# Moving 28 parts of a hand-written schedule: the scan layer's fronts, ends and early values, one at a time within or between its steps

## The chip, the cores and the metric

The kernel runs on one core of one Trainium2 chip. The metric is the device time of one execution in microseconds (us). The kernel before takes 5843.45 us, the median of three runs from 5842.38 to 5847.58. Engines are called as the profile calls them: PE (TensorE matmul; PEld is its weight load), DVE (VectorE), ACT (ScalarE), POOL (GpSimd) and SP, the queue that issues nearly all DMAs.

## The reference

Two layers in float32 on x, 4 images of 384 channels and 64x64 pixels. Each normalises its input in groups (32 groups) and adds its result to it: `x = x + layer(gn(x))`.

Layer 0 is a Mamba block on the 4096 tokens of an image. The change is in this layer:

```python
xn = (xs - mu) * rsqrt(var + 1e-05) * ln_w + ln_b
xb, z = split(xn @ in_proj_w.T)                 # 2 x 768 channels
xc = silu(causal_conv(xb, 4 taps) + conv_b)
dt, Bm, Cm = split(xc @ x_proj_w.T)             # 24, 16, 16
dt = softplus(dt @ dt_w.T + dt_b)
h_t = exp(dt_t * A) * h_(t-1) + (dt_t * x_t) * B_t   # 768 x 16 states, t = 0..4095
y_t = h_t . C_t
out = ((y + xc * D) * silu(z)) @ out_proj_w.T
```

Layer 1 is outlook attention with 3x3 windows at stride 2: attention weights from the pooled pixels, values from a 3x3 convolution, a weighted sum folded back, and a projection. A part of its values is computed early, between the steps of layer 0; that is all of it that the change touches.

## The kernel before

**Tiles and steps.** `mamba_layer` (line 111) cuts the 4 x 4096 tokens into 68 chunks of 241 tokens. One scan instruction covers 32 channels x 16 states (128 partitions, four stretches of 242 columns, 968 in all); a step of the main loop (line 956) has two of them, and 12 steps make a chunk's 768 channels. I number a chunk's steps 0 to 11. All chunks run as a pipeline: while a chunk's 12 steps scan, later chunks are prepared (fronts), an earlier one is finished (ends), and layer 1's early values are computed (behinds).

What a step does for the scan itself, in its order on each engine: SP fetches `dxr` and `dtr` for coming steps (even steps, `s_fetch` line 734 and `s_fetch_dt` line 743, four DMAs each); DVE writes half of the scan's input for the next step, `h<-dxr,bp` (`s_inputs2`, line 765), then runs two scans `h<-da,h` (`s_scan`, line 786); ACT copies the carried state (`s_carry`), makes the decays `da` of the next step in two groups of four exponentials (`s_decay`, line 774), each as soon as a scan has freed its buffer, and saves the state (`s_save`); POOL multiplies the scanned h of the step before by C, `h<-h,bc` (`s_outputs`, line 796), and writes the other half of the input two steps ahead, `h<-dxr,bc` (`s_inputs`, line 750); PE sums over states into y on odd steps (`s_sum`).

**What sets the order.** The order is written out by hand: each engine is wrapped in `InOrder` (line 38), which keeps its instructions in program order, so an instruction that waits holds everything behind it on its engine. Three tables say where other work goes. `plan` (line 608) holds the parts of a chunk's front, `ends` (line 642) its end, `behinds` (line 651) the early values. A key is a step, relative to the chunk, and one of six places in a step, EARLY, READY, SCAN, POOL, MID, LATE: before the next step's `h<-dxr,bp`; after it and before the scans; between the second scan and the second group of decays; after `h<-h,bc`; after `h<-dxr,bc` and PE's sum; last. Steps that differ by 12 fall on the same step of the loop for different chunks. `parts` (line 688) calls them, later chunks first. On an engine that a part doesn't use, its place means nothing; two places are the same for an engine that issues nothing between them.

**The parts** that matter below:

- the norm: `f_load`, `f_mean` (PE), `f_center` (DVE), `f_square` (ACT, line 312, 128x723), `f_var` (PE), `f_root` and `f_pow` (ACT: logarithm, then exponential, in place of a root), `f_scale` (DVE);
- projections and convolution: `f_x`, `f_z`, `f_conv` (PE, with ACT evictions), three of each; `f_gates` (ACT: two table loads and the Silu activations);
- `f_bc`, `f_xd` (line 447: ACT copies `xd`, SP stores it as `bcd`), `f_spread` (line 486: SP reads `bcd` back, eight DMAs), `f_dt`, `f_plog`, `f_log` (ACT), and `f_dtx` (line 512): DVE multiplies dt by xc for two of the six channel blocks, SP stores the product with four DMAs. Its tile has two buffers for three products of a chunk:

```python
def f_dtx(c, jj):
    if jj == 0:
        c.dxd = dram.tile([NJ, CG, 4, TM], F32, tag="dxd", name="dxd")
    dtx = front.tile([P, 2, TM], F32, tag="dtx", name="dtx", bufs=2)
    ve.tensor_mul(dtx, c.pl[jj], c.xc[jj][:, :, 1:])
    store(dtx, c.dxd[2 * jj : 2 * jj + 2])
```

- the ends: `e_load` (SP: `xr<-in_x`), `e_project` (PE and ACT: `ps_out`, `xr`), `e_mean`, `e_store` (SP: `x1<-xr`);
- the early values: `v_load` (line 534; SP loads the pixels of the next pair of tiles, `xo<-x1`, in three parts, in the chunk before the pair), `v_norm`, `v_begin`, `v_item` (PE `ps_v`, ACT `v<-ps_v`), `v_next` (line 596; SP stores `ve<-v` and fetches `wq`). Pairs of tiles start in chunks 20, 24, 28, 32, 37, 41, 45, 49, 54, 58 and 62 and last four chunks each.

Of the kernel before, what the change touches and what calls it, by code (L numbers as in the profile page):

```python
# [110 lines left out]
def mamba_layer(ctx, tc, x, w, x1, sc1, bi1, bi4, consts, early, behind):  # L111
# [410 lines left out]
    EARLY, READY, SCAN, POOL, MID, LATE = range(6)  # L522

    def at(f, *args):
        def part(c):
            f(c, *args)

        part.f = f
        return part
# [66 lines left out]
    def v_next(ch, n):  # L596
# [9 lines left out]
                    v_fetch(q + 1, cb)  # L606

    plan = {
        (-2, LATE): [f_load],
        (1, READY): [f_mean],  # L610
        (1, POOL): [f_center],
        (3, EARLY): [f_square],
        (3, POOL): [f_var],
        (3, LATE): [f_root],
        (4, READY): [f_pow],
        (4, POOL): [f_scale],
        (7, MID): [at(f_x, 0)],
        (8, EARLY): [at(f_x, 1)],
        (8, MID): [at(f_z, 0)],
        (9, MID): [at(f_conv, 0)],  # L620
        (10, SCAN): [at(f_z, 1)],
        (10, LATE): [at(f_z, 2)],
        (11, SCAN): [at(f_conv, 1)],
        (13, READY): [at(f_x, 2)],
        (13, MID): [at(f_conv, 2)],
        (13, LATE): [f_gates],
        (14, READY): [f_bc],
        (14, POOL): [f_xd],
        (15, SCAN): [at(f_dt, 0)],
        (15, POOL): [at(f_dt, 1)],  # L630
        (15, LATE): [f_column],
        (16, LATE): [at(f_dt, 2), at(f_plog, 0)],
        (17, EARLY): [f_spread],
        (17, LATE): [at(f_plog, 1)],
        (18, EARLY): [at(f_dtx, 0)],
        (18, READY): [at(f_plog, 2), at(f_dtx, 1), f_log],
        (19, READY): [at(f_dtx, 2)],
        (22, SCAN): [f_b],
        (25, LATE): [f_last],
    }  # L640

    ends = {
        (-4, SCAN): [lambda c: e_load(c)],
        (2, POOL): [lambda c: e_project(c, 0)],
        (5, MID): [lambda c: e_project(c, 1)],
        (6, SCAN): [lambda c: e_project(c, 2)],
        (7, READY): [lambda c: e_mean(c)],
        (7, MID): [lambda c: e_store(c)],
    }

    behinds = {
        (0, SCAN): [at(v_item, 0)],
        (1, READY): [at(v_next, 0)],
        (2, EARLY): [at(v_item, 1)],
        (3, POOL): [at(v_next, 1)],
        (4, SCAN): [at(v_item, 2)],
        (5, POOL): [at(v_next, 2)],
        (5, LATE): [at(v_item, 3)],
        (7, EARLY): [at(v_next, 3)],
        (8, SCAN): [at(v_load, 0)],  # L660
        (8, LATE): [at(v_item, 4)],
        (9, POOL): [at(v_load, 1)],
        (9, MID): [at(v_next, 4)],
        (10, READY): [at(v_load, 2)],
        (10, LATE): [at(v_norm, 0)],
        (11, EARLY): [v_begin],
        (11, MID): [at(v_norm, 1), at(v_norm, 2)],
    }

    def chunk(k):  # L670
# [160 lines left out]
    def e_tokens(c, v):  # L831

        return v[c.b, :, c.t0 - 1 + c.lo : c.t0 - 1 + TM].rearrange("(p cb) l -> p cb l", cb=NCB)

    def e_load(c):
        c.lo = 1 if c.ci == 0 else 0
        c.xr = io.tile([P, NCB, XT], F32, tag="xr", name="xr")
        sp.dma_start(c.xr[:, :, c.lo : TM], e_tokens(c, x))

    def e_project(c, cb):  # L840
        lo = c.lo
        po = pmm.tile([P, 2, TM], F32, tag="mm", name="ps_out")
        pe.matmul(po[:, 0, lo:], ident, c.xr[:, cb, lo:TM], start=True, stop=False)
        for j in range(NJ):
            pe.matmul(po[:, 0, lo:], wout[:, j, cb, :], c.zs[:, j, lo:TM], start=False, stop=(j == NJ - 1))
        if cb == 0:
            c.sums = small.tile([P, NCB], F32, tag="sums", name="sums")
        ae.activation(c.xr[:, cb, lo:TM], po[:, 0, lo:], AF.Identity, accum_out=c.sums[:, cb : cb + 1])

    def e_mean(c):  # L850


        n = TM - c.lo
        if c.ci == 0:
            st1[c.b] = small.tile([P, NC, 3], F32, tag="st1", name="st1")
            gp.memset(st1[c.b][:, 0:1, 0:1], float(NCB * n))
            gp.memset(st1[c.b][:, 1:, 0:1], float(NCB * TM))
        ae.activation(
            c.sums,
            c.sums,  # L860
            AF.Identity,
            scale=1.0 / (NCB * n),
            accum_out=st1[c.b][:, c.ci, 1:2],
        )

    def e_store(c):
        n = TM - c.lo
        ae.activation(
            c.zs[:, :NCB, :n],
            c.xr[:, :, c.lo : TM],  # L870
            AF.Square,
            scale=-1.0,
            bias=st1[c.b][:, c.ci, 1:2],
            accum_out=st1[c.b][:, c.ci, 2:3],
        )
        sp.dma_start(e_tokens(c, x1), c.xr[:, :, c.lo : TM])
        if c.ci == NC - 1:
            b = c.b
            made = group_norm_coeffs(
                pe, ve, ae, gp, small, pmm, blk4, mhalf, [st1[b].rearrange("p a s -> p (a s)")], sc1[:, b : b + 1], bi1[:, b : b + 1]  # L880
            )
            def parts():
                yield from made
                ae.mul(bi4[:, b : b + 1], bi1[:, b : b + 1], 4.0)

            norms.append([parts(), False])
# [655 lines left out]
def layers(ctx, tc, w, out):  # L1542
# [35 lines left out]

    started = []
    mamba_layer(tc, x.rearrange("b c h w -> b c (h w)"), w, x1, sc1, bi1, bi4, consts, early, behind)  # L1580
    outlook_layer(tc, x1, w, out, sc1, bi1, bi4, weights, ready, tiles)

# [67 lines left out]
```

## Time and profile before

| what | us |
|---|---|
| median of three runs | 5843.45 |
| the profiled execution, its own time | 5847.81 |
| its span | 5846.0 |
| first scan starts, last scan starts | 94.67, 4936.06 |
| one chunk, from first scan to first scan, chunks 1 to 19 (mean) | 70.6 |
| the same, the 40 chunks with early values under way (mean) | 71.3 |
| a scan on DVE, 128x968 | 2.15 |
| `h<-dxr,bp` on DVE, 128x964 | 1.13 |
| `dtx<-ps_lg,xc` on DVE, 128x482 | 0.65 |
| `h<-h,bc` on POOL, 128x1928 | 3.97 |
| `h<-dxr,bc` on POOL, 128x964 | 2.00 |
| four exponentials of `da` on ACT, 128x241 each | 1.62 |
| `sq<-u,bc` on ACT, 128x723 | 0.89 |

How to read it: the profile is one execution, taken by the hardware profiler. A row of a timeline says when an instruction started (us from the span's start), how long it took, its engine, and in square brackets how long the engine had been idle and what ended that. SPq rows are DMA issues, of which x4 means four in a row. A row of the waits view says who waited for whom: us in total, times, longest. All instructions that pass through `InOrder` carry its line, L53, so groups are told apart by their tiles.

### The profile page before, as it was taken

How to read it: one execution, taken by the hardware profiler on the slowest of the kernel's cores; microseconds unless marked ns; L12 is line 12 of the kernel's file. 1: busy time of each engine (PE TensorE's matmuls, PEld its weight loads, DVE VectorE, ACT ScalarE, POOL GpSimd, SP SyncE). 2: the span in 40 equal slices, each digit the busy share in tenths (PEclk: the TensorE clock that was granted, in tenths of full speed). 3: DMA queues.
4: the chain of work that ended last, by engine and by line, in shares of the span. 5: the costliest groups of instructions: out<-in, count | busy, mean ns of one | idle time of the engine just before them, and what ended most of it. 6: DMA issues, size and time to landing. Idle time of an engine off the chain costs nothing.

```text
span 5846.0 us, 126302 instructions
## 1 busy us (share of the span) xinstructions
PE 5294.4 (91%) x46156; PEld 3831.6 (66%) x46156; DVE 5248.9 (90%) x4267; ACT 4834.3 (83%) x13288; POOL 5404.3 (92%) x2051
## 2 busy tenths in 40 slices
PE   7888888888999999998999999999999996899999
PEld 6666666666666666666666666666666664567655
DVE  4999999999999999999999999999999998588644
ACT  4888888888888888888888888888889886577665
POOL 4999999999999999999999999999999998799733
PEclk9999999999999999999999999999999998999999
DMA  4555555555667666666666666656666656666554
GB/s 146 143 143 144 143 139 134 130 132 135 167 170 180 173 177 163 173 171 160 172 177 175 178 169 174 170 148 171 169 166 172 162 149 170 187 210 214 173 168 150
DMA packets 761512, 956.85 MB, mean 164 GB/s; under 512 B 211839, under 2 KB 663609, under 8 KB 760761
## 3 DMA queue, kind: packets, MB, share of 16 engines
q1 hardware_dynamic: 758296, 945.24, 59.6%
q8 instruction: 362, 5.93, 0.4%
q10 hardware_dynamic: 2592, 3.54, 0.2%
q14 instruction: 262, 2.14, 0.1%
HBM read 722.67 MB, written 225.70 MB: 162 GB/s over the span
## 4 chain that ended last, share of the span: by engine, by line
ACT 24%; PE 22%; DVE 8%; DMA 5%; POOL 4%; issue 4%; SPq 3%; ACTq 0%; DVEq 0%; POOLq 0%
ACT da L53 13%; DVE h L53 5%; PE ps_in L53 4%; PE ps_v L53 3%; SPq L53 3%; POOL h L53 3%; PE y L53 3%; PE psv L53 3%; PE ps L53 2%; PE pso L53 2%; PE psa L53 2%; PE ps_cv L53 2%; ACT L53 2%; DMA dtr<-dtd 1%; ACT xc L53 1%
## 5 line engine op out<-in xcount | busy, mean ns | idle before, releaser
L53 DVE TENSOR_TENSOR_SCAN h<-da,h 128x968 f32<-128x968 f32 x1632 | 3451.3, 2154 | 150.0 <-POOL h L53 73.5
L53 POOL TENSOR_TENSOR h<-h,bc 128x1928 f32<-128x1928 f32 x816 | 3240.9, 3972 | 41.5 <-DVE h L53 37.8
L53 ACT ACTIVATE da<-dtr,alog 128x241 f32<-128x241 f32 x6528 | 2644.7, 453 | 362.5 <-DVE h L53 290.1
L53 POOL TENSOR_TENSOR h<-dxr,bc 128x964 f32<-128x964 f32 x816 | 1633.2, 2001 | 57.3 <-issue 37.9
L53 PE MATMUL ps_in<-u,win 128*128 128x241 f32 x4824 | 1060.3, 371 | 44.7 <-ACT xb L53 28.9
L53 PEld LDWEIGHTS ps_in<-u,win 128*128 128x128 f32 x4824 | 907.0, 191 | 170.5 <-ACT xb L53 51.6
L53 DVE TENSOR_TENSOR h<-dxr,bp 128x964 f32<-128x964 f32 x816 | 925.2, 1134 | 4.9 <-DMA dxr<-dxd 3.6
L53 PE MATMUL y<-h,ssum 128*32 128x241 f32 x13056 | 777.8, 372 | 50.8 <-POOL h L53 50.7
L53 PE MATMUL ps_cv<-xb,cdiag 128*128 128x241 f32 x3264 | 718.7, 373 | 27.9 <-ACT zs L53 21.6
L53 PEld LDWEIGHTS ps_cv<-xb,cdiag 128*128 128x128 f32 x3264 | 606.5, 190 | 135.2 <-issue 34.8
L53 PEld LDWEIGHTS y<-h,ssum 128*32 128x32 f32 x13056 | 435.1, 111 | 317.9 <-POOL h L53 69.8
L53 POOL TENSOR_TENSOR bd<-ain,own 99x1188 f32<-99x1188 f32 x192 | 432.7, 2277 | 171.9 <-PE ps L53 156.9
L53 PE MATMUL ps_out<-zs,wout 128*128 128x241 f32 (+1 forms) x2448 | 564.4, 382 | 5.8 <-DVE zs L53 5.8
L53 ACT ACTIVATE bd<-ain,own 99x216 f32<-99x216 f32 (+1 forms) x1408 | 463.4, 417 | 92.1 <-PE ps L53 82.6
L53 PEld LDWEIGHTS ps_out<-zs,wout 128*128 128x128 f32 x2448 | 489.0, 200 | 49.1 <-DVE zs L53 6.2
L53 PE MATMUL ps_v<-wq,xo 128*32 128x384 f32 x4752 | 424.2, 489 | 31.9 <-ACT xr L53 30.1
L53 DVE TENSOR_TENSOR fold<-fold,ps 128x192 f32<-128x192 f32 (+1 forms) x768 | 210.1, 302 | 161.0 <-PE ps L53 136.5
L53 PE MATMUL ps_dt<-xd,wdt 128*128 128x241 f32 x816 | 227.6, 404 | 93.4 <-ACT xd L53 56.8
L53 PEld LDWEIGHTS ps_v<-wq,xo 128*32 128x32 f32 x4752 | 141.7, 110 | 238.2 <-issue 161.9
L53 PE MATMUL pso<-fold,wpr 128*128 128x256 f32 (+6 forms) x1026 | 279.4, 419 | 3.7 <-DVE fold L53 3.3
L53 PE MATMUL ps<-bd,vin 99*32 99x99 f32 (+1 forms) x9216 | 228.3, 250 | 43.6 <-DVE fold L53 20.4
L53 PEld LDWEIGHTS ps<-bd,vin 99*32 99x32 f32 (+1 forms) x9216 | 200.9, 110 | 98.2 <-issue 38.6
(132 smaller groups left out, 5554.6 us busy)
## 6 DMA issues: line engine op xcount, KB each, us to landing
dxr<-dxd SPq DMA_DIRECT2D x1632, 120.5 KB
dtr<-dtd SPq DMA_DIRECT2D x1632, 120.5 KB
wq<-in_wv SPq DMA_DIRECT2D x297, 192.0 KB
dxd<-dtx SPq DMA_DIRECT2D x816, 60.2 KB
dtd<-dt SPq DMA_DIRECT2D x272, 180.8 KB
ve<-v SPq DMA_DIRECT2D x198, 192.0 KB
bc<-bcd SPq DMA_DIRECT2D x272, 120.5 KB
vin<-ve SPq DMA_DIRECT2D x66, 445.5 KB
```

The lines of the kernel that those rows point to most:

```text
L53: made = self.tc.keep_in_program_order(issue(*args, **kwargs))
```

## The change

Only the three tables change: 28 entries stand at other places, and `f_root` shares one with `f_pow`. No instruction is added, removed or altered. The whole diff of the tables:

```diff
     plan = {
-        (-2, LATE): [f_load],
-        (1, READY): [f_mean],
+        (-1, EARLY): [f_load],
+        (0, LATE): [f_mean],
         (1, POOL): [f_center],
-        (3, EARLY): [f_square],
+        (2, POOL): [f_square],
         (3, POOL): [f_var],
-        (3, LATE): [f_root],
-        (4, READY): [f_pow],
-        (4, POOL): [f_scale],
+        (4, READY): [f_root, f_pow],
+        (4, MID): [f_scale],
         (7, MID): [at(f_x, 0)],
         (8, EARLY): [at(f_x, 1)],
-        (8, MID): [at(f_z, 0)],
+        (8, LATE): [at(f_z, 0)],
         (9, MID): [at(f_conv, 0)],
-        (10, SCAN): [at(f_z, 1)],
-        (10, LATE): [at(f_z, 2)],
+        (9, LATE): [at(f_z, 1)],
+        (11, EARLY): [at(f_z, 2)],
         (11, SCAN): [at(f_conv, 1)],
-        (13, READY): [at(f_x, 2)],
+        (12, MID): [at(f_x, 2)],
         (13, MID): [at(f_conv, 2)],
         (13, LATE): [f_gates],
-        (14, READY): [f_bc],
+        (14, EARLY): [f_bc],
         (14, POOL): [f_xd],
         (15, SCAN): [at(f_dt, 0)],
-        (15, POOL): [at(f_dt, 1)],
-        (15, LATE): [f_column],
-        (16, LATE): [at(f_dt, 2), at(f_plog, 0)],
-        (17, EARLY): [f_spread],
+        (15, POOL): [f_column, at(f_dt, 1)],
+        (16, SCAN): [f_spread],
+        (16, POOL): [at(f_dt, 2)],
+        (17, READY): [at(f_plog, 0)],
         (17, LATE): [at(f_plog, 1)],
         (18, EARLY): [at(f_dtx, 0)],
         (18, READY): [at(f_plog, 2), at(f_dtx, 1), f_log],
-        (19, READY): [at(f_dtx, 2)],
-        (22, SCAN): [f_b],
+        (18, POOL): [at(f_dtx, 2)],
+        (22, READY): [f_b],
         (25, LATE): [f_last],
     }
     ends = {
-        (-4, SCAN): [lambda c: e_load(c)],
+        (-3, POOL): [lambda c: e_load(c)],
...
-        (7, READY): [lambda c: e_mean(c)],
+        (7, EARLY): [lambda c: e_mean(c)],
         (7, MID): [lambda c: e_store(c)],
     }
     behinds = {
         (0, SCAN): [at(v_item, 0)],
         (1, READY): [at(v_next, 0)],
-        (2, EARLY): [at(v_item, 1)],
-        (3, POOL): [at(v_next, 1)],
+        (1, LATE): [at(v_item, 1)],
+        (3, EARLY): [at(v_next, 1)],
         (4, SCAN): [at(v_item, 2)],
-        (5, POOL): [at(v_next, 2)],
-        (5, LATE): [at(v_item, 3)],
-        (7, EARLY): [at(v_next, 3)],
-        (8, SCAN): [at(v_load, 0)],
-        (8, LATE): [at(v_item, 4)],
-        (9, POOL): [at(v_load, 1)],
-        (9, MID): [at(v_next, 4)],
-        (10, READY): [at(v_load, 2)],
-        (10, LATE): [at(v_norm, 0)],
-        (11, EARLY): [v_begin],
-        (11, MID): [at(v_norm, 1), at(v_norm, 2)],
+        (5, SCAN): [at(v_next, 2)],
+        (6, EARLY): [at(v_item, 3)],
+        (7, EARLY): [at(v_next, 3), at(v_load, 0)],
+        (8, LATE): [at(v_item, 4), at(v_load, 1)],
+        (9, LATE): [at(v_next, 4)],
+        (10, EARLY): [at(v_load, 2)],
+        (11, READY): [at(v_norm, 0)],
+        (11, POOL): [at(v_norm, 1)],
+        (11, MID): [v_begin, at(v_norm, 2)],
     }
```

## The prediction

> **What bounds the kernel now.** I read the page first. Four engines are busy for 83 to 92% of the span, and no group of part 5 has idle time worth the span before it, so the question is how tightly the engines hold each other in the scan loop.
>
> ```profile
> span 5846.0 us, 126302 instructions
> PE 5294.4 (91%) x46156; PEld 3831.6 (66%) x46156; DVE 5248.9 (90%) x4267; ACT 4834.3 (83%) x13288; POOL 5404.3 (92%) x2051
> ...
> L53 DVE TENSOR_TENSOR_SCAN h<-da,h 128x968 f32<-128x968 f32 x1632 | 3451.3, 2154 | 150.0 <-POOL h L53 73.5
> L53 POOL TENSOR_TENSOR h<-h,bc 128x1928 f32<-128x1928 f32 x816 | 3240.9, 3972 | 41.5 <-DVE h L53 37.8
> ```
>
> The scans start at 94.7 us and the last at 4936.1 us: 816 steps, 68 chunks of 12. From one chunk's first scan to the next one's takes 70.6 us (mean of chunks 1 to 19, without early values) and 71.3 us (mean of the 40 chunks with them). Next, three windows of one chunk each: one without early values, one with, and one in which a wait shows.
>
> ```profile
> 630.70:701.00 70.30, 60.51 (x442) 46.78 (x442) 68.88 (x47) 60.96 (x168) 70.12 (x25) 0.95 0.54 143
> 3093.90:3164.60 70.70, 66.75 (x554) 47.56 (x550) 68.77 (x47) 62.09 (x174) 69.54 (x25) 1.00 0.65 173
> 3164.60:3237.20 72.60, 67.69 (x574) 47.95 (x566) 69.10 (x48) 62.62 (x174) 70.55 (x25) 1.00 0.63 172
> ```
>
> Columns: window, length, busy PE, PEld, DVE, ACT, POOL. POOL has 0.2 to 2.1 us of idle time per chunk, DVE 1.4 to 3.5. Two engines are full at once, and what DVE loses in the wrong place POOL loses too. Where that place is, the timeline of the third window says (DVE, then POOL):
>
> ```profile
> 3206.73 1.13 DVE L53 TENSOR_TENSOR h<-dxr,bp 128x964 f32<-128x964 f32 x1
> 3209.43 0.66 DVE L53 TENSOR_TENSOR dtx<-ps_lg,xc 128x482 f32<-128x482 f32 x1 [1.57 <-DMA dxd<-dtx]
> 3210.01 4.22 DVE L53 TENSOR_TENSOR_SCAN h<-da,h 128x968 f32<-128x968 f32 x2
> ```
> ```profile
> 3210.91 1.98 POOL L53 TENSOR_TENSOR h<-dxr,bc 128x964 f32<-128x964 f32 x1
> 3214.38 3.94 POOL L53 TENSOR_TENSOR h<-h,bc 128x1928 f32<-128x1928 f32 x1 [1.49 <-DVE h L53]
> ```
>
> DVE waited 1.57 us for a transfer before the third dtx, POOL then 1.49 us for the scan, and this chunk took 72.5 us where its neighbours took 70.8. **A wait at the third dtx of a chunk is paid in full.** The waits view has ten of them (13.7 us); those ten chunks take 72.1 us on average, the other 30 with early values 71.0.
>
> The transfer is the store of the chunk's first dtx: two dtx buffers serve three products, so the third must wait until the first has left. When it leaves is up to SP, which issues everything in order. Chunk 26, with early values:
>
> ```profile
> 1967.55 0.77 SPq L53 DMA_DIRECT2D bcd<-xd  x2
> 1968.35 0.42 SPq L53 DMA_DIRECT2D ve<-v  x1
> 1968.87 1.12 SPq L53 DMA_DIRECT2D wq<-in_wv  x1
> 1970.11 2.45 SPq L53 DMA_DIRECT2D dxr<-dxd  x4
> 1972.60 1.98 SPq L53 DMA_DIRECT2D dtr<-dtd  x4
> 1974.68 0.37 SPq L53 DMA_DIRECT2D xs<-in_x  x1
> 1975.09 3.74 SPq L53 DMA_DIRECT2D bc<-bcd  x8
> 1978.93 0.38 SPq L53 DMA_DIRECT2D ve<-v  x1
> 1979.40 0.90 SPq L53 DMA_DIRECT2D wq<-in_wv  x2
> 1980.41 3.15 SPq L53 DMA_DIRECT2D dxr<-dxd  x4
> 1983.65 1.92 SPq L53 DMA_DIRECT2D dtr<-dtd  x4
> 1985.67 4.04 SPq L53 DMA_DIRECT2D dxd<-dtx  x8
> ```
>
> SP stands still until ACT has copied xd (828.8 us of such waits in 68 chunks), then issues 18 us without a pause. The first dtx ended at 1981.52; its store begins 4.2 us later only because SP gets there then. So **the store's landing hangs on when xd is copied**, not on dtx. In chunks without ve and wq SP comes 0.0 to 2.0 us after the dtx.
>
> From the trace I took, for 64 chunks, the landing of the first dtx's last store, from the end of that dtx. In the 24 chunks with no or few early values it is 3.10 to 5.43 us. In the other 40 it is 5.85 to 9.37, median 7.26, mean 7.46: 5 under 6.70, 24 between 6.70 and 7.72, 11 above.
>
> **The change part by part.** The two programs' instruction orders, put side by side engine by engine, differ little: most of the 28 parts pass nothing that is on their own engine (f_load, f_center, f_root, f_pow, f_scale, f_dt, f_plog, f_spread, f_b, e_mean, e_load, nearly all of v_item and v_next). In a chunk of the steady loop this remains:
>
> 1. DVE: the third dtx comes before the h<-dxr,bp of step 7, not after it.
> 2. ACT: the square (sq) comes before the xd copies of step 2, not after them and the eviction of ps_out.
> 3. SP: the third dtx's four stores come before v_next's ve and wq.
> 4. ACT: the two zs evictions of f_z(1) come before carry and decay of step 10.
> 5. PE: f_x(2) before f_mean.
> 6. ACT: the zs column copy before the second dt.
> 7. SP, in 11 chunks: two of the three xo loads come earlier, one ahead of the x1 store.
>
> *Part 1.* The scans of step 6 end 6.88 us after the first dtx. Before, h<-dxr,bp (1.13 us, 1.05 to the next start) runs there, and dtx starts at 7.84, or 0.12 us after the landing L if that is later. After, dtx may start at 6.80 or at L + 0.12, and h<-dxr,bp follows before the scan. The scan of step 7 is later by max(6.80, L + 0.12) + 1.05 - max(7.84, L + 0.12): nothing for L under 6.70, rising to 1.05 for L over 7.72. The cover that goes is the 1.05 us of work which stood ahead of the wait. At the median: 7.38 + 1.05 - 7.84 = 0.59; over the 40 chunks, one by one, 25.4 us. The other chunks have 1.3 us to spare and cost nothing.
>
> *Part 2.* sq takes 0.89 us and its input is ready 10 us before, so xd is copied 0.88 us later. ACT's own sum to the next decay is the same. But bcd, and with it SP's whole run down to dxd, starts 0.88 us later; in the rows above nothing in that run waits for anything else. L becomes L + 0.88: at the median 8.26 + 1.05 - 7.84 = 1.47, over the 40 chunks 58.5 us with part 1. The same lateness reaches wq (issued 1979.40), whose landing holds the early product and its copy (ACT waits 2.27 us for ps_v just before plog), and with them ACT's decay of step 7; that path would delay the same scan by about 0.9 us, so it lies under the 1.47 and is not added. In chunks without early values SP has idle time and L + 0.88 stays under 6.4: nothing. Bounds: SP may win the 0.88 back (25.4), or pass it on (58.5).
>
> What POOL can hide of it I took from its next h<-h,bc in the same chunks: it starts 0.00 to 0.14 us later than the scan's end allows in 33 of 40, 0.18 to 1.57 in seven. Subtracted one by one: 51.9 us with parts 1 and 2, 20.8 with part 1 alone.
>
> A rule speaks against part 1: the Trainium skill, "DMA: Bandwidth & Descriptors", Rules for kernel authors, says to issue early and wait on the semaphore late, and this waits earlier. By the rule alone all 64 chunks would pay 1.05 us (67 us, an estimate); by the landings 24 of them pay nothing. [...]
>
> *Part 3* lets ve and wq (0.4 to 1.4 us of issue) leave 1.8 us later; the early product that uses them begins over 2 us after their landing (51 against 53 us into the chunk). Nothing; without that cover up to 1 us of PE in a chunk. *Part 4* puts 0.80 us ahead of a decay whose scan starts 1.4 us after its end: nothing, at worst 0.3 us in a chunk. *Part 5* brings the xb copy, for which ACT waits 1.24 us (54.8 us in all), forward by about that. But the second decay behind it starts at 1955.82 and cannot before the scan ends at 1955.67: 0.09 us a chunk, 64 times, 5.8 us gained. *Part 6* is 0.20 us between neighbours whose sum is unchanged: nothing. *Part 7*: an xo load of 544 KB takes 5.6 to 6.8 us to land, and now stands ahead of the dtr that ACT needs in step 9; in these 11 chunks dtr lands 0.1 to 3.7 us before ACT starts on it, and the decay could start 1.9 us later without holding the scan. Between -0.9 us (DVE's idle time at the start of the next chunk) and +3 for each; I take +0.5, nearer to the dtr row, 5.5 us in all.
>
> **Sum**, against the profiled execution (span 5846.0, its own time 5847.8): + 51.9 - 5.8 + 5.5 = 5899.4. It stood 4.4 us over the median 5843.45, so I say **5895 us**, 0.9% slower.
>
> **The rivals.** *SP catches up* (part 1 alone): 5847.8 + 20.8 - 5.8 + 5.5 - 4.4 = 5864. For it: L spreads over 3.5 us, so SP's queue is not rigid; against it: no pause in the 18 us. *Faster*: part 5 is worth more than I say. ACT's run of gates in steps 1 and 2 (two table loads, six activations) ends DVE's longest stall, 1.0 to 1.5 us before the scan of step 3, and xb starts that run. If the run gains half of the 54.8 us that ACT waits for xb, and DVE's third dtx is hidden by POOL's 70 us, the time is 5816. It decides if the scan that holds the second decay comes earlier too; the 0.15 us between its end and the decay's start speak against it. *No difference*: the moves compensate, for instance a later xd and an earlier xb; within 12 us of 5843. That the change does little is likely for most parts, as the orders show, but not for 1 and 2.
>
> **How the numbers follow.** Mine (5868 to 5930) 0.57; SP catches up 0.14; no difference 0.11; faster 0.18. Slower by over 0.2% (11.7 us, about what can be told from no change) is 0.57 + 0.14 = 0.71. The range runs from 5836, in the case of no difference, to 5930: with 58.5 unhidden, part 4 at its 0.3 us in 64 chunks and part 7 at 0.5, 5847.8 + 58.5 + 19 + 5.5 - 4.4 = 5926, and a little of part 7's upper end. That leaves out the faster case in the main.
>
> **What would show it.** Right: waits of DVE dtx for DMA dxd<-dtx grow from 13.7 us in 10 to some 50 us or more in over 30; bcd<-xd is issued 0.9 us later after the decay of step 2; POOL's h<-h,bc of step 7 waits for DVE about 1 us in chunks 20 to 64; chunks 1 to 19 keep their 70.6 us. Part 2 is wrong if SP's dxd comes as long after the dtx as now. All of it is wrong if those waits stay near 14 us, or if they grow and the chunks do not.

## The result and the profile after

The changed kernel takes 5917.22 us (median of four runs, 5912.38 to 5924.86) against 5842.91 of the kernel before (four runs on the same chip): ratio 1.0126, 95% interval 1.0114 to 1.0139, **74 us slower**. The prediction said 5895, so the direction and the mechanism stood, and a third of the move was missing.

The page of the changed kernel, its span and its two largest groups:

```profile
span 5910.6 us, 126217 instructions
PE 5287.0 (89%) x46156; PEld 3846.3 (65%) x46156; DVE 5250.1 (89%) x4267; ACT 4843.9 (82%) x13288; POOL 5405.5 (91%) x2051
...
L53 DVE TENSOR_TENSOR_SCAN h<-da,h 128x968 f32<-128x968 f32 x1632 | 3452.8, 2156 | 145.5 <-POOL h L53 65.9
L53 POOL TENSOR_TENSOR h<-h,bc 128x1928 f32<-128x1928 f32 x816 | 3243.4, 3975 | 100.3 <-DVE h L53 89.3
```

The engines are busy for as long as before (DVE 5250.1 us against 5248.9, POOL 5405.5 against 5404.3): nothing runs longer, all of the 64.6 us of span is waiting. POOL's waits for DVE's scans went from 37.8 us to 89.3. From the first scan to the last it takes 61.4 us more. The chunks 1 to 19 keep their length (70.59 us, 70.64 before); the chunks 20 to 64 take 72.87 us on average, against 71.44. Three windows of one chunk each, chunks 8, 42 and 43 (window, length, busy PE, PEld, DVE, ACT, POOL, granted clock, DMA share, GB/s):

```profile
664.91:735.55 70.64, 60.46 (x444) 46.99 (x443) 69.01 (x47) 61.04 (x169) 70.64 (x25) 0.95 0.55 140
3122.19:3195.26 73.07, 67.10 (x570) 48.23 (x566) 69.01 (x47) 62.79 (x175) 69.00 (x24) 1.00 0.63 168
3195.26:3270.52 75.26, 68.88 (x566) 49.16 (x562) 69.22 (x48) 62.54 (x174) 71.77 (x26) 0.98 0.62 166
```

Chunk 42 has grown from 70.8 us to 73.07 and chunk 43 from 72.5 to 75.26, with nearly the same busy time on DVE. It is not the clock granted to PE: chunk 42 has 1.00 in both kernels and grew by 2.2 us. The waits view says which waits grew (us in total, times, longest); three lines of the kernel before, then the changed kernel:

```profile
ACT xb L53 <- PE ps_in L53: 54.8, 40, 4.5
ACT zs L53 <- PE ps_in L53: 15.1, 21, 5.1
DVE dtx L53 <- DMA dxd<-dtx: 13.7, 10, 4.7
```
```profile
ACT da L53 <- DVE h L53: 332.3, 508, 3.6
POOL h L53 <- DVE h L53: 89.3, 88, 3.7
PE ps_in L53 <- ACT xb L53: 79.9, 55, 4.7
ACT zs L53 <- PE ps_in L53: 63.9, 53, 4.7
ACT da L53 <- DMA dtr<-dtd: 58.9, 28, 4.3
DVE dtx L53 <- DMA dxd<-dtx: 56.9, 36, 4.7
ACT xb L53 <- PE ps_in L53: 12.5, 11, 4.1
DVE h L53 <- PE bp L53: 5.7, 6, 1.4
```

The third dtx's wait for the first one's store went from 13.7 us in 10 places to 56.9 in 36. The view puts some waits of the third dtx down to ACT, seven of them in the changed kernel, though there too the dtx began 0.08 to 0.22 us after the store's landing; with those the third dtx waits 67.9 us in 43 places, 14.6 in 12 before. Chunk 26, DVE's rows around its third dtx, then POOL's:

```profile
1989.45 4.23 DVE L53 TENSOR_TENSOR_SCAN h<-da,h 128x968 f32<-128x968 f32 x2
1995.93 0.66 DVE L53 TENSOR_TENSOR dtx<-ps_lg,xc 128x482 f32<-128x482 f32 x1 [2.25 <-DMA dxd<-dtx]
1996.51 1.15 DVE L53 TENSOR_TENSOR h<-dxr,bp 128x964 f32<-128x964 f32 x1
1997.57 4.23 DVE L53 TENSOR_TENSOR_SCAN h<-da,h 128x968 f32<-128x968 f32 x2
```
```profile
1997.77 1.98 POOL L53 TENSOR_TENSOR h<-dxr,bc 128x964 f32<-128x964 f32 x1
2001.95 3.94 POOL L53 TENSOR_TENSOR h<-h,bc 128x1928 f32<-128x1928 f32 x1 [2.20 <-DVE h L53]
```

DVE stands for 2.25 us with `h<-dxr,bp` ready behind the wait; POOL, which must multiply what the scan leaves, stands 2.20 us a little later. The store's way there, SP's rows in the same chunk:

```profile
1973.62 0.77 SPq L53 DMA_DIRECT2D bcd<-xd  x2
...
1981.17 3.74 SPq L53 DMA_DIRECT2D bc<-bcd  x8
1985.01 0.38 SPq L53 DMA_DIRECT2D ve<-v  x1
1985.49 2.25 SPq L53 DMA_DIRECT2D wq<-in_wv  x2
1987.84 2.46 SPq L53 DMA_DIRECT2D dxr<-dxd  x4
1990.39 1.92 SPq L53 DMA_DIRECT2D dtr<-dtd  x4
1992.41 3.71 SPq L53 DMA_DIRECT2D dxd<-dtx  x8
```

Still no pause between `bcd` and `dxd`. Measured from the start of step 3's scans, `bcd` is issued 2.88 us into the step (median of chunks 20 to 64), 2.09 before: 0.79 us later. The landing of the store, from the end of the first dtx, has its median at 8.00 us in these chunks, 7.21 before: again 0.79 to 0.80 us later. SP gave nothing back.

### The profile page after: what moved, and what is told of

It is laid out like the page before. It is cut to its first block, busy times and chain, and to the rows that moved or that the text cites. A ratio compares the mean times of both kernels' runs of the same rounds, so it can differ in the third digit from the quotient of the medians.

```text
span 5910.6 us, 126217 instructions
## 1 busy us (share of the span) xinstructions
PE 5287.0 (89%) x46156; PEld 3846.3 (65%) x46156; DVE 5250.1 (89%) x4267; ACT 4843.9 (82%) x13288; POOL 5405.5 (91%) x2051
## 4 chain that ended last, share of the span: by engine, by line
ACT 25%; PE 20%; DVE 11%; SPq 6%; DMA 5%; POOL 5%; issue 5%; DVEq 0%; ACTq 0%; POOLq 0%
ACT da L53 14%; DVE h L53 8%; SPq L53 6%; POOL h L53 4%; PE ps_in L53 3%; PE psv L53 3%; PE y L53 2%; PE ps_cv L53 2%; PE ps_v L53 2%; ACT zs L53 2%; PE ps L53 2%; PE psa L53 2%; PE pso L53 2%; ACT L53 2%; DMA dtr<-dtd 2%
## 5 line engine op out<-in xcount | busy, mean ns | idle before, releaser
L53 POOL TENSOR_TENSOR h<-h,bc 128x1928 f32<-128x1928 f32 x816 | 3243.4, 3975 | 100.3 <-DVE h L53 89.3
L53 PE MATMUL ps_in<-u,win 128*128 128x241 f32 x4824 | 1074.0, 374 | 96.4 <-ACT xb L53 79.9
L53 PEld LDWEIGHTS ps_dt<-xd,wdt 128*128 128x128 f32 x816 | 146.8, 198 | 202.2 <-ACT xd L53 123.0
```

The costliest lines, as they stand in the source:

```text
L53: made = self.tc.keep_in_program_order(issue(*args, **kwargs))
```

## The experiments

All ratios are against the kernel before, run on the same chip beside it, with 95% intervals; (ratio - 1) x 5843 gives the us. The changed kernel stands at 1.0126, + 74 us. The medians of the kernel before lay between 5837 and 5846 from chip to chip and hour to hour, and its profiled execution (5847.8) lay above all of them, so a difference between two traces is some 2 to 11 us smaller than the one between the medians.

**Undoing the third dtx and the square, one at a time and together.** On the changed kernel; the first pair of lines is a_dtx_back, the second a_sq_back, a_both_back has both:

```diff
-        (18, POOL): [at(f_dtx, 2)],
+        (19, READY): [at(f_dtx, 2)],
-        (2, POOL): [f_square],
+        (3, EARLY): [f_square],
```

> The changed kernel with the third dtx back behind h<-dxr,bp. Theory (the wait for the first dtx's store is paid because nothing stands ahead of it): by the landings of before, 0.88 us later, the old place costs 19.4 us over the kernel before, the new one 58.5; less what POOL hides, some 37 us come back: 5917 becomes about 5880, and the waits of dtx for dxd<-dtx fall from 56.9 us to about 25. Rival (the time was lost elsewhere, at the gates' and z's matmuls, and the wait only moved): under 10 us come back, 5907 or more.

> The changed kernel with the square back behind the xd copies. Theory (the square makes xd, bcd and with them SP's whole run 0.88 us later, and the landing with it): part 1 alone remains of the two, 20.8 us in place of 51.9, so 31 us come back: about 5886; the issue of dxd comes some 0.8 us earlier after the first dtx than in the changed kernel. Rival (SP wins the 0.88 us back on its way): the time stays at 5917 and dxd comes as late as it does now.

> The changed kernel with both back. Theory: the 51.9 us of the two go, about 5865 remains, and the 22 us still above the kernel before belong to the other parts, f_z(1) ahead of the decay of step 10 first of all. Rival (the two parts are all of it and were priced too low): 5843 within 6 us.

Measured: a_dtx_back 1.0055 (1.0042 to 1.0067), + 32 us; a_sq_back 1.0055 (1.0043 to 1.0068), + 32 us; a_both_back 1.0014 (1.0005 to 1.0023), + 8 us. The wait in each, by the waits views, in the same order:

```profile
DVE dtx L53 <- DMA dxd<-dtx: 26.3, 19, 4.9
```
```profile
DVE dtx L53 <- DMA dxd<-dtx: 26.2, 26, 4.4
```
```profile
DVE dtx L53 <- DMA dxd<-dtx: 13.3, 9, 4.7
POOL h L53 <- DVE h L53: 43.3, 66, 5.4
```

All waits of the third dtx together are 30.6, 36.6 and 14.5 us, so the square by itself adds 16 us, the dtx's move by itself 22, and both add 53: either alone is partly covered, by the landing that comes earlier or by the 1.05 us of work ahead of the wait. With the square back, the issue of `dxd` is at 3.55 us after the first dtx (median of chunks 20 to 64), 4.34 in the changed kernel. So the rivals "the wait only moved" and "SP wins it back" both fall. The two parts together carry 65 us (1.0126 - 1.0014), not 52.

**The two alone, on the kernel before** (the same two entries, changed there).

> The kernel before with parts 1 and 2 alone (third dtx ahead of h<-dxr,bp, square ahead of the xd copies). Prediction: + 51.9 us, POOL hiding 6.6 of the 58.5 that the landings give. If POOL hides nothing: + 58.5. If taking the two back from the changed kernel is the measure: + 64. If a third part is needed for the cost (f_z(1) or the x1 stores of the ends): under 45.

Measured: 1.0111 (1.0098 to 1.0125), + 65 us. No third part is needed. Its waits view:

```profile
PE ps_in L53 <- ACT xb L53: 77.2, 53, 4.7
DVE dtx L53 <- DMA dxd<-dtx: 44.6, 29, 4.5
DVE h L53 <- PE bp L53: 8.2, 9, 1.4
```

Two things are to be seen. Over the chunks 5 to 65, DVE has 50.8 us more idle time than before, 45.2 of it behind step 6, where the third dtx stands, and these chunks take 55.2 us longer together. And there is a wait that the kernel before doesn't have, DVE's for `bp`. It sits in the same chunk, four steps behind the late dtx, and brings 8.2 us of DVE's idle time.

**f_z(1) behind the decay of step 10 again.** On the changed kernel:

```diff
-        (9, LATE): [at(f_z, 1)],
+        (10, SCAN): [at(f_z, 1)],
```

> The changed kernel with f_z(1) back behind the decay of step 10. By the prediction's part 4 (hidden) nothing changes: 5917. Theory formed from the trace after (ACT stands for f_z(1)'s matmul ahead of carry and decay of step 10, its waits for ps_in grew from 15.1 to 63.9 us, and DVE newly waits 13.6 us in step 10): 12 to 20 us come back, 5897 to 5905, and DVE's waits in step 10 go to about nothing.

Measured: 1.0097 (1.0084 to 1.0111), so 17 us come back, not cleanly known (the two intervals allow 6 to 28).

```profile
PE ps_in L53 <- ACT xb L53: 80.6, 52, 4.7
ACT zs L53 <- PE ps_in L53: 13.0, 11, 3.7
```

ACT's wait for the z matmuls is gone, and so is DVE's for `bp`. One reservation: `f_b` was moved by the change from SCAN to READY of the same step, so in this kernel PE runs `bp` ahead of f_z(1)'s matmuls, an order that neither kernel has. The 17 us are for both.

**The store earlier, the tables untouched.** On the changed kernel, and on the one before; in step 6 alone, `s_fetch` (dxr, due four steps later) goes behind the first dtx's stores:

```diff
-        if m % 2 == 0 and s > -4 and unit(s + 4) is not None:
+        if m % 2 == 0 and m != 6 and s > -4 and unit(s + 4) is not None:
             s_fetch(s + 4)
...
         parts(s, EARLY)
+        if m == 6 and unit(s + 4) is not None:
+            s_fetch(s + 4)
```

> The changed kernel, its three tables untouched, but in step 6 of each chunk SP fetches dxr (used four steps later) after the first dtx's stores instead of before them. Theory (the landing of that store is what costs): the store leaves 2.5 to 3.2 us earlier, the landing falls under 6.8 us in nearly every chunk, the waits of dtx fall from 56.9 us to under 10, and the 64 us that the third dtx and the square cost together come back nearly whole: about 5855, though both stay where the change put them. Rival (the order on DVE and ACT itself costs, not the transfer): 5900 or more. Third way: POOL then waits for the late dxr, seen as POOL h waiting for dxr<-dxd, and the time stays.

Measured: 1.0059 (1.0046 to 1.0073), so 39 us of the 74 come back, with the third dtx and the square where the change put them. The landing's median falls from 7.99 to 5.69 us (chunks 20 to 65), and the waits of dtx nearly vanish; but ACT's waits for `dtr` grow from 58.9 us, and DVE's idle time before its scans, put to "issue" by the view, from 62.7:

```profile
ACT da L53 <- DMA dtr<-dtd: 128.3, 42, 5.6
DVE h L53 <- issue: 98.4, 84, 3.3
DVE dtx L53 <- DMA dxd<-dtx: 5.4, 4, 4.3
```

The expected 5855 was missed because a wait stood behind the one removed: ACT's decay of step 9 needs the `dtr` that SP fetches in step 8, and with SP's run still late by the square this `dtr` is now what ends last. DVE's idle time behind step 9 goes from 6.4 us to 27.2. Chunk 42, ACT, then DVE, which needs this decay:

```profile
3165.47 1.62 ACT L53 ACTIVATE da<-dtr,alog 128x241 f32<-128x241 f32 x4 [4.64 <-DMA dtr<-dtd]
```
```profile
3167.18 4.24 DVE L53 TENSOR_TENSOR_SCAN h<-da,h 128x968 f32<-128x968 f32 x2 [2.48 <-issue]
```

So the landing is shown to cost more than half of the change. That the square's lateness has a second way to the scan is read from the traces, which agree on it: DVE's idle time behind step 9 is 21.0 us in a_dtx_back, where the square is early, 8.1 in a_both_back, and 2.9 with the same exchange on SP and the square in its old place (the next run). In the changed kernel, where the scans come late anyway, it is 6.4.

> The kernel before with the same exchange on SP. Theory: the ten waits of dtx for dxd<-dtx (13.7 us) go, and since such a wait is paid in full the time falls by 10 to 14 us, 5846 to about 5834. Rival (those waits lie beside POOL's work): no change within 6 us.

Measured: 1.0004 (0.9995 to 1.0013), no change. The waits of dtx fell from 13.7 us in 10 to 6.4 in 2, and at most 3 us were gained for the 7.3 us of wait:

```profile
DVE dtx L53 <- DMA dxd<-dtx: 6.4, 2, 4.8
```

One wait of 4.7 or 4.8 us, at 80 us, stands ahead of the first scan in both kernels; in the loop the waits fell from 9.0 us in 9 places to 1.6 in one.

**Part 5 alone**, on the kernel before:

```diff
-        (1, READY): [f_mean],
+        (0, LATE): [f_mean],
-        (13, READY): [at(f_x, 2)],
+        (12, MID): [at(f_x, 2)],
```

> The kernel before with part 5 alone: f_x(2) ahead of f_mean on PE. By the prediction: ACT's wait for f_x(2), 54.8 us in all, goes almost whole, and 5.8 us are gained, 5846 to 5840. Rival (faster: half of that wait is passed on): about 5819. Rival (nothing is passed on): 5846 within 4 us.

Measured: 0.9984 (0.9975 to 0.9992), 9 us faster (5 to 15). ACT's wait for f_x(2) went as foreseen, from 54.8 us in 40 places:

```profile
ACT xb L53 <- PE ps_in L53: 12.4, 11, 3.9
```

**What is left: three parts back, then four.** The changed kernel with the third dtx, the square and f_z(1) back; and, in a_four_back, the loads of the next pair's pixels too:

```diff
-        (7, EARLY): [at(v_next, 3), at(v_load, 0)],
-        (8, LATE): [at(v_item, 4), at(v_load, 1)],
-        (10, EARLY): [at(v_load, 2)],
+        (7, EARLY): [at(v_next, 3)],
+        (8, SCAN): [at(v_load, 0)],
+        (8, LATE): [at(v_item, 4)],
+        (9, POOL): [at(v_load, 1)],
+        (10, READY): [at(v_load, 2)],
```

> The changed kernel with the third dtx, the square and f_z(1) all back: what the other 25 parts do. By the prediction's terms (parts 5 and 7) 5846 - 5.8 + 5.5, no change from the kernel before. If the 13 us of f_z(1) add to the two others: 5853 - 13 = 5840. If f_z(1) only costs where the other two have made the chunk late: 5853, as without it.

> The changed kernel with the third dtx, the square, f_z(1) and the loads of the next pair's pixels back. Against the run with three back this is part 7. Prediction: 5.5 us less (0.5 in each of 11 chunks), which is what f_x(2) ahead of f_mean gave alone, 0.9984 of the kernel before. If the loads cost nothing: 0.9996, as with three back.

Measured: three back 0.9996 (0.9987 to 1.0004), - 2 us; four back 0.9982 (0.9974 to 0.9991), - 11 us. f_z(1) costs 10 us here as well, where the two big parts are gone (1.0014 to 0.9996; with the intervals some 3 to 18). The loads cost 8 us (1 to 15); in the traces the 11 chunks that load take 71.02 us with three back and 70.57 with four, + 0.45 us each. Four back is b_x2 again within the error: all the other entries of the change together are worth what part 5 is, within some 7 us.

**Two versions meant to beat both**, on b_x2: the third dtx behind the scans of step 7, its stores behind the fetches of step 8; and `s_fetch_dt` ahead of `s_fetch` in every even step.

```diff
-        (19, READY): [at(f_dtx, 2)],
+        (19, SCAN): [at(f_dtx, 2)],
+        (20, EARLY): [at(f_dtx_out, 2)],
```

> A version that may beat both: the kernel before with f_x(2) ahead of f_mean, the third dtx behind the scans of step 7 and its stores behind the fetches of step 8. Theory: the last waits for the first dtx's store (14.2 us with f_x(2) alone) go to zero, 0.9984 becomes some 0.9975. Rival (the dtr of step 9 is the next wait, and holds what the other gave): no change from 0.9984. Rival (the third ps_lg is held 5 us longer and f_x(1) waits for it): slower than 0.9984.

Measured: 0.9998 (0.9989 to 1.0006); the gain of part 5 is lost again. The third case came:

```profile
ACT xb L53 <- PE ps_in L53: 40.9, 91, 4.1
DVE dtx L53 <- DMA dxd<-dtx: 5.1, 1, 5.1
```

The wait for the store is gone but for one, and ACT waits for f_x's matmul 91 times instead of 11. That the buffer in PSUM (the memory PE writes to) that the third `ps_lg` holds for longer does it fits the count, but wasn't tested by itself.

> A version that may beat both: the kernel before with f_x(2) ahead of f_mean, and SP fetching dtr (due in two steps) ahead of dxr (due in four) in every even step. Theory: ACT's 66.3 us of waits for dtr, nearly all in step 9, fall by 2.4 us each to under 15 us; DVE stands only some 2 to 6 us of that, so 0.9984 becomes 0.9975 at best. Rival: the dxr comes late for POOL, slower.

Measured: 0.9986 (0.9977 to 0.9995), no change against b_x2. ACT's wait for `dtr` in b_x2, then this run:

```profile
ACT da L53 <- DMA dtr<-dtd: 66.3, 39, 3.0
```
```profile
ACT da L53 <- DVE h L53: 359.9, 625, 2.8
ACT da L53 <- DMA dtr<-dtd: 1.4, 1, 1.4
```

65 us of ACT's waits for `dtr` vanished, ACT now waits for DVE's scans instead (318.7 us in b_x2), and the time stayed. The fastest kernels of this study are the one before with part 5 alone and the changed one with four parts back, 9 and 11 us under the kernel before.

## Why the prediction was right, and where its sizes were off

*What bounds it.* The place was right: the third dtx's wait for the first one's store. "A wait at the third dtx of a chunk is paid in full" was not right as it was argued. Ten slow chunks with a wait were compared with thirty without; b_dxr6_late took eight of the view's ten waits away and gained 3 us at most. The correlation was no price. (The view's ten are not quite the ten chunks either: its largest, 4.7 us, lies ahead of the first scan, and the waits of two of the chunks, 38 and 39, are put to ACT.) For the waits that the change adds, though, the price is more than in full: in b_two the third dtx waits 46.7 us more than before, by all its waits, and the chunks 5 to 65 take 55.2 us longer.

*Parts 1 and 2* (+ 51.9 net, 58.5 before POOL's share): measured + 65, by adding them alone (57 to 73) and by taking them back. The lateness of SP's run was right: 0.79 us against the 0.88 of the prediction, and the landing took it over whole (0.80). Its effect at the dtx was close, too: DVE's idle time behind step 6 grew by 52.4 us in the trace of the changed kernel. Two things were wrong.

First, **the step that subtracted what POOL can hide** (6.6 us). It counted the places in which POOL's `h<-h,bc` starts later than the scan allows. In b_two, over the chunks 5 to 65, DVE's idle time grew by 45.2 us behind step 6 and by 8.2 behind step 10, and the chunks took 55.2 us longer: the loop took the whole lateness over, with nothing taken off. (That POOL's idle time grew by 52.7 us there, or by 62.5 in the changed kernel, is no proof by itself, since any engine with unchanged work stands longer in a longer loop.) Why POOL's slack in that step gave no cover was not tested.

Second, the sum **ended at the scan of step 7**. The late scan goes on. Chunk 43 shows the chain, ACT, PE, and DVE:

```profile
3244.14 1.62 ACT L53 ACTIVATE da<-dtr,alog 128x241 f32<-128x241 f32 x4 [2.53 <-DVE h L53]
...
3247.86 0.55 ACT L53 COPY xb<-ps_in 128x482 f32<-128x482 f32 x1
...
3262.81 0.82 ACT L53 ACTIVATE zs<-ps_in,bxz 128x241 f32<-128x241 f32 x2 [1.55 <-PE ps_in L53]
```
```profile
3248.46 4.29 PE L53 MATMUL ps_in<-u,win 128*128 128x241 f32 x12 [2.44 <-ACT xb L53]
...
3262.61 0.97 PE L53 MATMUL bp<-xd,sel 128*128 128x241 f32 x4
```
```profile
3263.62 1.16 DVE L53 TENSOR_TENSOR h<-dxr,bp 128x964 f32<-128x964 f32 x1 [0.70 <-PE bp L53]
3265.31 4.24 DVE L53 TENSOR_TENSOR_SCAN h<-da,h 128x968 f32<-128x968 f32 x2 [0.54 <-ACT da L53]
```

ACT waits 2.53 us for the late scan, so f_x(0)'s copy comes late; PE waits 2.44 us for it and from there runs without a pause through v_item, y, f_conv, f_z(1) to `bp`, and DVE, which needs `bp` for the next chunk's first input, stands a second time. DVE's idle time behind step 10 is 13.6 us in the changed kernel and 8.2 with the two parts alone; it was 0.0. That is a second payment for the same delay, and the prediction had no term for it. The chain is read from the trace; that `bp` ahead of f_z(1) on PE removes it, a_z1_back shows, though with f_z(1) moved on ACT at the same time.

*The rival "SP catches up"* is refuted by the landing's 0.80 us and by a_sq_back. *The rule weighed in part 1*: the Trainium skill, "DMA: Bandwidth & Descriptors", Rules for kernel authors, says to wait on a DMA's semaphore late, and the runs agree with its direction: the earlier wait alone costs 24 us (1.0055 - 1.0014, with the square back; 15 to 33). The page's rule has no size, and the 67 us worked out from it for all chunks would have come near for a wrong reason: the chunks 1 to 19 paid nothing.

*The second path of part 2* ("lies under the 1.47 and is not added") was right to leave out as long as the first one holds. a_dxr6_late shows one when the first is taken away; it goes by the `dtr` of step 9 in the main (27.2 us of DVE's idle time there, 6.4 in the changed kernel), and DVE stands another 10.2 us, in 12 places, before the scans of step 7, where the prediction looked for it (1.7 in one in the changed kernel).

*Part 4* (nothing, at worst 0.3 a chunk, 19 in all): 10 to 17 us, with `f_b`'s order in it. The step that failed put only ACT's own 0.80 us ahead of the decay, and not the wait for PE which that eviction has in front of it: `zs <- ps_in` from 15.1 us to 63.9. *Part 5* (- 5.8): - 9, with 5.8 inside the interval; its rival at 5816 falls, since of 42 us of wait removed about a fifth reached the end. *Part 7* (+ 0.5 a load): + 0.45 by the traces, + 8 us by the medians. *Parts 3 and 6* and the rest: nothing clear of the error of some 7 us, by four back against b_x2.

The sum by the runs: 65 - 9 + 8 + 10 = 74, and 74 was measured. Taking parts back one after another must add up to the whole; what was tested by itself is that the two parts alone give the same 65 (b_two) and part 5 alone the - 9 (b_x2). The forecast's 5895 lacked 13 us at parts 1 and 2 and 10 at part 4; its errors at parts 5 and 7, about 3 us each, happened to cancel, which is luck.

## What to carry to other kernels

In a kernel that issues its transfers in order, follow a moved instruction through the queue to the last transfer behind it: 0.79 us of lateness at the head came out as 0.80 us eighteen microseconds later, and what was a hidden landing became a wait. Price the new wait by what stands behind it on its engine, and then go on past the first late instruction: ask which engine waits for that one, and whether one with no idle time carries the delay to the next critical place. And don't read a price off slow chunks that happen to contain a wait; take the wait away.

## What the runs showed that was not expected

What waits cost is not their total, and it can be less or more. 65 us of ACT's waits for `dtr` could be removed for no gain, and 7 us of DVE's for 3 at most; the 47 us that b_two adds to the waits of the third dtx cost 55 us in the traces and 65 by the medians. Two parts that each cost 24 us alone (a_sq_back and a_dtx_back over a_both_back) cost 65 together: each uses up a cover that the other needs.

The time from the issue of the first of the four stores to the landing of the last varies from chunk to chunk: in chunk 25 of the changed kernel the four landed 7.24, 7.44, 9.29 and 9.47 us after the dtx, in chunk 29 at 7.38, 7.59, 7.80 and 8.16, with nearly the same issue times (4.45 and 5.00 for the first). The third dtx began 0.12 us after the last one in both.
